# Two attention and two expert stages on one core: loads, last rows and router pieces moved where stages meet, a token's two result rows side by side, end sums on three engines

## The chip, the cores and the metric

The kernel runs on one core of a Trainium2 chip, as one launch. The metric is device time in microseconds (us). The profile adds one execution of the same program, taken apart by the hardware profiler. Five engines matter: TensorE (PE in the profile; its weight loads are PEld), VectorE (DVE), ScalarE (ACT), GpSimd (POOL) and SyncE (SP). SP, ACT and POOL also issue DMA transfers; each engine takes its instructions strictly in order, so an instruction that waits holds up all that stand behind it on that engine, DMA issues included.

## The reference

The input x is 8 batches of 512 tokens of width 256, in float32. Four layers follow, each with a residual:

```
x = x + attn_a(layernorm(x))     # 16 heads of 64, ALiBi, causal softmax, bias
x = x + ffn(layernorm(x))        # RMS norm, gate, top 2 of 8 experts, swiglu
x = x + attn_b(layernorm(x))     # 8 heads of 128, rotary, causal softmax
x = x + ffn(layernorm(x))        # the same expert weights again
```

In the expert layer each token's normed row h goes to the two experts with the largest gate logits. An expert computes a 256x512 product, a clipped swiglu and a 256x256 product. The residual of the inner layer is h's own input, so the layer's output is the token's x plus two expert rows, each times a softmax weight.

## The kernel before

Everything is float32 except the router's small one-hot tables. Tokens are laid on 128 partitions, so a batch has 4 token tiles of 128 rows.

**Attention** (class `Attention`, kinds "a" and "b") goes through 64 steps, a step being 2 heads of kind "a" or 1 head of kind "b" in one batch. A step of kind "a" (`step`, L503) issues on PE the scores of its own heads, then the transposes of the softmax rows of the step before (`turn`), the projections q and k of the step after, and the weighted sums of the step before (`average`). `extra(1)` and `extra(2)` are slots for other work: values, output projection, the next batch's norm, the router. Within one step the scores go from PSUM through DVE (L407: add the mask, take the row maximum), ACT (L417: exp and row sum), then a reciprocal on DVE and the scaling of the rows on DVE (the longest rows of a step; all rows in the very last step) and POOL (L434). The transposed rows come from PSUM through ACT, one of six banks through DVE (L457 and L459).

**Experts** (class `Experts`, kinds "f1" and "f2"). After each attention batch `norm`, `apply`, `turn_norm`, `gates`, `choose` and `count` make the router's input; `sorting` turns the choices into slots: all (token, choice) pairs are sorted by expert into blocks of 128 rows, padded, 71 blocks (TOTAL). The work has two stages: 41 blocks (FULL) hold pairs of batches 0 to 5 and can start before the router has seen batches 6 and 7; 30 blocks come after, and rows of batches 0 to 5 can lie in the first 55 blocks (TOUCHED). `tokens` (L891) computes for each slot which token's row to gather and to which row of the DRAM tensor `y_all` the result goes. `run` (L1049) is a software pipeline over n: at n it gathers block n+4 (`gather`, an indirect DMA on POOL), transposes the activations of block n-5, transposes the gathered rows of block n (`turn_rows`), does the first product of block n-2 (`first`) and the second of block n-6 (`second`, which ends with an indirect DMA on POOL that scatters 128 rows to `y_all`). The dictionary `aside` puts other pieces behind given values of n.

In `turn_rows` the transposed rows of the first AHEAD blocks are copied back into the tile they were gathered to; later blocks use a tile that shares its memory with the attention's output tile O, and so wait until the last output projection has read O.

**What sets the order.** PE's order is the program order. The other engines' instructions are put in order by a planner, which simulates the program with its own costs and takes the earliest written of those it holds ready; instructions marked `keep_in_program_order` stay in order. The order is fixed at build time: if a transfer takes longer on the chip than in the plan, the engine waits with what stands first.

**Where stages meet.** `layer` (L1133) spreads the router's pieces over the attention steps by batch, head group and slot. Pieces that fall behind the last batch are returned in `left`: the last step's transposes (`turn_last`), its weighted sum (`average`), two pieces of output projection, then norm, apply, turn_norm, gates, choose and count of batch 7. `flush` (L1195) puts these ten pieces at n = 0, 2, 2, 2, 3, 5, 8, 10, 12, 14 of the expert pipeline and the six sorting pieces of the second stage at 16, 18, 20, 22, 25, 28.

**Loads at the start.** Input DMAs stand on SP in the order of the code (L146 to L175): x of batch 0, wq, wk, alibi, bout, wv, wo, small tables, then 16 transfers of expert weights (`we`, 6 MB), sin. x of batch 1 is loaded by `fetch_a(0)` at slot (0, 1, 1), behind those. `fold_norm` scales the expert weights on POOL as they arrive (L243).

**Result rows.** `y_all` has two planes of 4096 rows, one for a token's first expert and one for its second, then spare rows for padding. `collect` (L1097) reads a tile's or half batch's rows back with one DMA from each plane (`read`, L1076); `add` (L1112) adds each row times its weight to x, one DVE instruction (L1118) per token tile and plane. For f1 the sums are made during attention b, one token tile per step; for f2, twelve half batches of batches 0 to 5 are summed from n = 61 on, and the four half batches of batches 6 and 7 at the very end, each followed by its store to the output (L1246).

## Time and profile before

| what | value |
|---|---|
| median of 3 runs | 2254.11 us (2252.29 to 2255.5) |
| the profiled execution's own time | 2239.6 us |
| span of that execution, first to last instruction | 2237.8 us |
| mean granted TensorE clock | 0.993 |
| PE busy | 2190.3 us, 98% of the span |
| DVE busy | 1586.9 us, 71% |
| ACT busy | 961.6 us, 43% |
| POOL busy | 967.1 us, 43% |
| DMA | 108.80 MB, mean 49 GB/s |

Times in the profile count from the start of the span. "Releaser" in brackets names what ended an engine's idle time before an instruction. Attention a lies at 0 to 927 us, f1 to 1175, attention b to 1976, f2 to the end. The PE clock row is the share of full clock that was granted.

### The profile page before, as it was taken

Reading aid. Unit: us, or ns where it says so; the run is one execution under the profiler, and the core shown is the slowest. Engines: PE = TensorE matmul, PEld = TensorE weight load, DVE = VectorE, ACT = ScalarE, POOL = GpSimd, SP = SyncE. Lnnn points to the kernel's source line nnn. Section 1 sums busy time; section 2 is a strip of 40 time slices with the busy share of each in tenths; the row PEclk is TensorE's granted clock in tenths of the full one; section 3 lists DMA queues with packets and bytes.
Section 4 is the critical chain, followed back from the end, with each engine's and each line's share of the span. In section 5 each row is a group of like instructions: output and inputs, shape, how many; then the busy total and the mean of one; then the engine's idle time right before and its main releaser. Section 6 shows DMA issues by size and latency. Waiting matters only on the chain.

```text
span 2237.8 us, 33567 instructions
## 1 busy us (share of the span) xinstructions
PE 2190.3 (98%) x10513; PEld 1429.2 (64%) x10513; DVE 1586.9 (71%) x4817; ACT 961.6 (43%) x2784; POOL 967.1 (43%) x1337
## 2 busy tenths in 40 slices
PE   8999999999999999999999999999999999999995
PEld 5666666666666666656666666666666666665663
DVE  4566666666666687687787676777777678968768
ACT  4555555555555555323324334434444433333331
POOL 5443434243433333266654343333434343356662
PEclk9999999999999999999999999999999999999997
DMA  7100000000000000232220010100101010042237
GB/s 248 39 15 15 6 24 1 30 1 29 1 29 1 29 6 29 99 106 84 90 76 29 10 39 10 39 29 19 48 6 43 6 34 1 19 139 78 85 101 252
DMA packets 78382, 108.80 MB, mean 49 GB/s; under 512 B 9568, under 2 KB 64000, under 8 KB 78208
## 3 DMA queue, kind: packets, MB, share of 16 engines
q1 hardware_dynamic: 62656, 67.58, 9.4%
q0 software_dynamic: 13632, 37.24, 5.4%
q8 instruction: 87, 1.43, 0.3%
q10 hardware_dynamic: 1920, 1.84, 0.3%
q14 instruction: 87, 0.71, 0.1%
HBM read 67.02 MB, written 39.60 MB: 48 GB/s over the span
## 4 chain that ended last, share of the span: by engine, by line
PE 88%; DVE 7%; issue 2%; ACT 1%; POOL 1%; SPq 1%; DMA 1%; DVEq 0%; ACTq 0%; POOLq 0%
PE pp_b L337 10%; PE hp_f L982 9%; PE pp_a L337 9%; PE op_a L476 6%; PE sp_b L395 6%; PE sp_a L395 6%; PE tp_a L449 6%; PE op_b L476 6%; PE yp_a L494 5%; PE yp_b L494 5%; PE vp_a L318 4%; PE y_f L1021 4%; PE vp_b L318 4%; PE tp_b L449 3%; PE gtp_f L953 1%
## 5 line engine op out<-in xcount | busy, mean ns | idle before, releaser
L417 ACT ACTIVATE S_a<-S_a,nm_a 128x512 f32<-128x512 f32 (+3 forms) x512 | 280.1, 548 | 313.7 <-DVE nm_a L407 309.9
L350 POOL TENSOR_TENSOR qk_b<-qk_b,rot_b 128x512 f32<-128x512 f32 x128 | 163.0, 1274 | 453.1 <-DVE qk_b L349 427.7
L376 POOL TENSOR_SCALAR ali_a<-alibi 128x512 f32<-128x512 f32 x128 | 79.3, 620 | 454.9 <-DVE nm_a L407 443.1
L982 PE MATMUL hp_f<-we,hT_f 128*128 x544 | 257.8, 596 | 4.3 <-DVE u_f L993 2.9
L417 ACT ACTIVATE S_b<-S_b,nm_b 128x512 f32<-128x512 f32 (+3 forms) x256 | 142.9, 559 | 241.1 <-DVE nm_b L407 233.4
L407 DVE CUSTOM_DVE_ANT_0 S_a<-sp_a,ali_a 128x512 f32<-128x512 f32 (+3 forms) x512 | 215.9, 487 | 30.7 <-PE sp_a L395 30.7
L434 POOL TENSOR_SCALAR S_a<-S_a,sum_a 128x384 f32<-128x384 f32 x378 | 203.1, 554 | 34.6 <-DVE sum_a L428 25.0
L1033 POOL DMA_INDIRECT y_f<-y_f,row_f x142 | 143.4, 1010 | 114.1 <-DVE y_f L1032 59.2
L407 DVE CUSTOM_DVE_ANT_0 S_b<-sp_b,mask 128x512 f32<-128x512 f32 (+3 forms) x256 | 119.4, 485 | 77.1 <-PE sp_b L395 76.7
L395 PE MATMUL sp_b<-qk_b 128*128 128x512 f32 (+3 forms) x512 | 169.7, 434 | 2.6 <-POOL qk_b L350 2.5
L449 PE MATMUL tp_a<-ident,S_a 128*128 128x128 f32 x1280 | 166.2, 276 | 5.4 <-DVE O_a L484 3.3
L939 POOL DMA_INDIRECT g_f<-h_all_f,token_f x142 | 144.4, 1017 | 59.4 <-issue 39.6
L449 PEld LDWEIGHTS tp_a<-ident,S_a 128*128 128x128 f32 x1280 | 141.3, 142 | 36.8 <-issue 21.3
L994 ACT ACTIVATE u_f<-u_f 128x256 f32<-128x256 f32 x142 | 59.2, 417 | 238.0 <-DVE u_f L993 179.5
L476 PE MATMUL op_a<-PT_a,V_a 128*64 128x384 f32 (+3 forms) x1024 | 156.0, 442 | 3.3 <-ACT S_a L417 2.2
L1021 PEld LDWEIGHTS y_f<-we,aT_f 128*128 128x128 f32 x568 | 108.8, 193 | 77.1 <-issue 59.6
L395 PE MATMUL sp_a<-qk_a 64*128 64x512 f32 (+3 forms) x1024 | 155.5, 443 | 0.9 <-DVE qk_a L354 0.9
L1021 PE MATMUL y_f<-we,aT_f 128*128 x568 | 148.6, 385 | 3.8 <-ACT aT_f L1012 3.7
L459 ACT COPY PT_a<-tp_a 128x512 f32<-128x512 f32 (+1 forms) x320 | 139.1, 496 | 29.4 <-PE tp_a L449 27.6
L476 PE MATMUL op_b<-PT_b,V_b 128*128 128x512 f32 (+3 forms) x512 | 148.7, 433 | 0.0
L993 DVE TENSOR_TENSOR u_f<-hp_f,be 128x512 f32<-128x512 f32 x142 | 98.2, 691 | 59.5 <-PE hp_f L982 20.5
L982 PEld LDWEIGHTS hp_f<-we,hT_f 128*128 128x128 f32 x544 | 92.7, 190 | 73.1 <-issue 66.3
(205 smaller groups left out, 4454.8 us busy)
## 6 DMA issues: line engine op xcount, KB each, us to landing
h_all_f<-hn_f SPq DMA_DIRECT2D x64, 128.0 KB
xm_f<-x_mid_f SPq DMA_DIRECT2D x16, 512.0 KB
yg_f<-y_f SPq DMA_DIRECT2D x32, 256.0 KB
yg_f<-y_f SPq DMA_DIRECT2D x56, 128.0 KB
we<-w_dram SPq DMA_DIRECT2D x8, 512.0 KB
x_mid_f<-x SPq DMA_DIRECT2D x8, 512.0 KB
x_mid_f<-xm_f SPq DMA_DIRECT2D x8, 512.0 KB
x<-x_in_dram SPq DMA_DIRECT2D x7, 512.0 KB
```

The lines of the kernel that those rows point to most:

```text
L318: nc.tensor.matmul(vp[:, k, :], lhsT=self.xT[b][:, c, t * P : (t + 1) * P], rhs=wv[:, c, q * 2 * P : (q + 1) * 2 * P], start=(c == 0), sto ...
L337: nc.tensor.matmul(pp, lhsT=w[:, c, g * P : (g + 1) * P], rhs=self.xT[b][:, c, :], start=(c == 0), stop=(c == NC - 1),)
L350: nc.gpsimd.tensor_tensor(qk[:, j, :], qk[:, j, :], rot, ALU.add)
L395: nc.tensor.matmul(sp[i][:, at[it] : at[it] + w], lhsT=qk[r, 0, it * P : (it + 1) * P], rhs=qk[r, 1, 0:w], start=True, stop=True,)
L407: nc.vector.tensor_tensor_reduce(out=s, in0=sp[i][:, at[it] : at[it] + w], in1=add[i][:, T - w : T], scale=scale, scalar=float(np.finfo(np ...
L417: nc.scalar.activation(s, s, AF.Exp, bias=nm[:, it : it + 1], scale=-1.0, accum_out=sums[:, it : it + 1],)
L434: eng.tensor_scalar(s, s, sums[:, it : it + 1], 1.0, ALU.mult, ALU.mult)
L449: nc.tensor.transpose(tp[:, o : o + P], S[:, S_OFF[it] + jt * P : S_OFF[it] + (jt + 1) * P], ident,)
L476: nc.tensor.matmul(op[i * cols : (i + 1) * cols, jt * P : T], lhsT=v[:, jt, c0 : c0 + cols], rhs=PT[i][:, P_OFF[jt] : P_OFF[jt] + T - jt * P],
L494: nc.tensor.matmul(yp[:, 0:D], lhsT=o[:, c, t * P : (t + 1) * P], rhs=wo[:, half * HALF + c, :], start=(c == 0), stop=(c == HALF - 1),)
L982: nc.tensor.matmul(hp, lhsT=h[:, c * P : (c + 1) * P], rhs=we_sb[:, bass.DynSlice(wat + c * 2 * FI, 2 * FI)], start=(c == 0), stop=(c == N ...
L1021: nc.tensor.matmul(yp, lhsT=aT[:, c * P : (c + 1) * P], rhs=we_sb[:, bass.DynSlice(wat + NC * 2 * FI + c * D, D)], start=(c == 0), stop=(c ...
```

## The change

It has these parts; no arithmetic of a result is changed but the place of a sum.

1. wq and wk of attention a are loaded in two pieces each: the first 256 columns of both, then alibi, then the other 768 columns.
2. x of batch 1 is loaded on SP before the expert weights; `fetch_a` goes on with batch 2.
3. In the last step of attention a the transposes of the step before come first, then the scores of the last step; then the extra slots and the weighted sum.
4. `flush` puts the ten pieces at 2, 4, 4, 4, 5, 7, 10, 12, 14, 17 and the sorting pieces at 18, 20, 22, 24, 26, 29, after both attentions. AHEAD goes from 3 to 5.
5. A token's two rows stand next to each other in `y_all` (rows 2t and 2t+1, spare rows from 8192 on). `tokens` computes this with one DVE instruction more, the gather's index before the scatter's. `collect` reads both rows with one DMA, in runs of 2 KB where two DMAs had runs of 1 KB.
6. For the last three of the twelve half batches and for the last four of f2, the second row's product goes to ACT and its sum to POOL; DVE keeps the first row. The last four reads go alternately to SP and ACT, one DMA each, where each had one on either queue.

```diff
-AHEAD = 3
+AHEAD = 5
...
+    def load_qk(first, end):
+        for k, w in enumerate((wq, wk)):
+            nc.sync.dma_start(
+                out=w[:, :, first:end],
+                in_=by_rows(a_qkv[:, k * INNER + first : k * INNER + end]),
+            )
+
+    load_qk(0, 2 * P)
     alibi_sb = load(const, [P, T], alibi, "alibi", "bias")
+    load_qk(2 * P, INNER)
...
     rank_sb = load(const, [P, NT, NE], rank, "rank")
+    X[1] = load_x(x_in[1], "x1")
...
-            if self.kind == "a":
+            if self.kind == "a" and not after:
+
+                turn(0, 0, 1, 2)
+                turn(1, 0, 1, 2)
+                for n in range(3):
+                    scores(n)
+                extra(1)
+                extra(2)
+            elif self.kind == "a":
...
+            nc.vector.scalar_tensor_tensor(
+                row_f, token_f, float(P), place, ALU.mult, ALU.add
+            )
+            nc.vector.tensor_scalar(token_f, mark, 96.0, 1.0, ALU.is_ge, ALU.mult)
+            nc.vector.scalar_tensor_tensor(
+                row_f, row_f, 2.0, token_f, ALU.mult, ALU.add
+            )
...
-                out=out, in_=self.y_all[first : first + n, :].rearrange("(t p) d -> p t d", p=P)
+                out=out,
+                in_=self.y_all[2 * first : 2 * (first + n), :].rearrange(
+                    "(t p k) d -> p t k d", p=P, k=2
+                ),
...
-            for k in range(2):
-                self.read(engines[k], b, got[:, k], k * PLANE + m * P, len(tiles) * P)
+            self.read(engine, b, got, m * P, len(tiles) * P)
...
                 for k in range(2):
-                    made = nc.vector.scalar_tensor_tensor(
-                        xs, got[:, k, n, :], self.R["w"][k][:, m : m + 1], xs, ALU.mult, ALU.add
-                    )
+                    row, w = got[:, n, k, :], self.R["w"][k][:, m : m + 1]
+                    if k and shared:
+
+                        nc.scalar.mul(row, row, w)
+                        nc.gpsimd.tensor_tensor(xs, xs, row, ALU.add)
+                        continue
+                    made = nc.vector.scalar_tensor_tensor(xs, row, w, xs, ALU.mult, ALU.add)
...
-        turns = (0, 2, 2, 2, 3, 5, 8, 10, 12, 14)
+        turns = (2, 4, 4, 4, 5, 7, 10, 12, 14, 17)
...
-        for n, piece in zip((16, 18, 20, 22, 25, 28), exp.sorting(1), strict=True):
+        for n, piece in zip((18, 20, 22, 24, 26, 29), exp.sorting(1), strict=True):
...
-    more += [((b, 1, 1), lambda b=b: fetch_a(b + 1)) for b in range(NB - 1)]
+    more += [((b, 1, 1), lambda b=b: fetch_a(b + 1)) for b in range(1, NB - 1)]
...
-        aside.setdefault(n + 4, []).append(lambda b=b, tt=tt: exp_b.add(b, tt))
+        aside.setdefault(n + 4, []).append(
+            lambda b=b, tt=tt, k=k: exp_b.add(b, tt, k >= len(halves) - 3)
+        )
...
-    for b, tt in last:
-        exp_b.collect(b, tt, "S", (nc.sync, nc.scalar))
+    for k, (b, tt) in enumerate(last):
+        exp_b.collect(b, tt, "S", (nc.sync, nc.scalar)[k % 2])
...
-        exp_b.add(b, tt)
+        exp_b.add(b, tt, True)
```

## The prediction

> **What bounds the kernel now.** I read the page first: PE works almost without a break, so only PE's work or its few gaps can be won, plus the ends of the span.
>
> ```profile
> PE 2190.3 (98%) x10513; PEld 1429.2 (64%) x10513; DVE 1586.9 (71%) x4817; ACT 961.6 (43%) x2784; POOL 967.1 (43%) x1337
> PE   8999999999999999999999999999999999999995
> PEclk9999999999999999999999999999999999999997
> ```
>
> The change takes no matmul away, so the 47.5 us in which PE is idle (2237.8 less 2190.3) and the time at a lowered clock are all there is to win. The table by stretches says where they are (columns: stretch, length, busy us of PE, PEld, DVE, ACT, POOL, granted clock, DMA share, GB/s).
>
> ```profile
> 0.00:30.00 30.00, 24.80 (x109) 16.02 (x110) 14.12 (x59) 12.47 (x37) 16.57 (x38) 1.00 0.94 316
> 30.00:60.00 30.00, 26.96 (x137) 15.59 (x136) 15.25 (x54) 13.61 (x41) 16.70 (x29) 0.94 0.48 146
> 920.00:960.00 40.00, 37.43 (x182) 23.86 (x183) 26.54 (x74) 15.31 (x44) 15.77 (x19) 0.96 0.33 108
> 1180.00:1900.00 720.00, 717.12 (x3057) 481.97 (x3057) 530.99 (x1454) 288.76 (x759) 278.46 (x349) 1.00 0.07 23
> 2200.00:2238.00 38.00, 14.16 (x46) 9.03 (x44) 31.80 (x77) 3.63 (x11) 7.97 (x8) 0.69 0.77 249
> ```
>
> Attention b is closed (2.9 us open of 720); the start, the meeting of attention a and f1, and the end are open. Third, the timeline of each. At the start, SP, DVE and PE:
>
> ```profile
> 31.16 0.37 SPq L134 DMA_DIRECT2D x<-x_in_dram  x1
> ...
> 39.63 0.75 DVE L253 BATCH_NORM_STATS2 st_a<-x 128x6 f32<-128x256 f32 x2 [5.30 <-DMA x<-x_in_dram]
> ...
> 42.01 1.04 PE L449 MATMUL tp_a<-ident,S_a 128*128 128x128 f32 x6 [2.56 <-DVE O_a L484]
> 43.23 3.26 PE L337 MATMUL pp_a<-xT_a,wq_a 128*128 128x512 f32 x4 [0.17 <-DVE nm_a L407]
> ```
>
> x of batch 1 is issued at 31.16 behind the expert weights and lands at 39.6. The planner had put its statistics ahead of DVE's next work, so DVE stands 5.30 us with scores and copies behind, and PE stands too, then runs slowly (3.26 us for four matmuls that take 1.88 later).
>
> At 920, ACT and PE:
>
> ```profile
> 926.26 1.32 ACT L459 COPY PT_a<-tp_a 128x512 f32<-128x512 f32 x3
> ...
> 926.88 1.07 PE L476 MATMUL op_a<-PT_a,V_a 128*64 128x512 f32 x2 [2.23 <-ACT S_a L417]
> 928.28 3.82 PE L476 MATMUL op_a<-PT_a,V_a 128*64 128x512 f32 x14 [0.34 <-issue]
> ```
>
> The last step's scores come first, so ACT's exps (921.89 to 926.3) stand ahead of the copies that the weighted sum needs.
>
> At the end PE stops at 2217.8 and DVE adds rows without a break, 33 times 0.46 us, to 2234.34; the last store and its landing take 3.46 us more.
>
> ```profile
> 2219.20 15.14 DVE L1118 SCALAR_TENSOR_TENSOR xm_f<-yg_f,wt_f,xm_f 128x256 f32<-128x256 f32 x33
> 2222.59 2.11 ACTq L1078 DMA_DIRECT2D yg_f<-y_f  x4
> ```
>
> **The change part by part**, against the profiled execution's own 2239.6 us (14.5 below the median, which I take off at the end).
>
> *Batch 1's x ahead of the expert weights.* Scores of step 2 start at 35.84, those of step 3 at 55.40: 19.56 us. The same kind of step in batch 4 takes 13.89 (chain, 466.39 to 480.28). Excess 5.67, gap and slow clock together: it goes if x is there in time. x takes the place of the first expert weight, whose first use on POOL starts on its landing, at 20.93. Its eight statistics instructions take 1.75 us (39.63 to 41.38). In DVE's order they should now fall after step 0's scores (end 19.18): waiting to 20.93 and ending at 22.68, they put the 1.54 us of reciprocals and scalings that stood at 20.55 to 22.09 and the q/k copy (22.37) to 24.2 to 24.9. PE's next scores need that copy by 23.99, so PE waits +0.9. Bounds: 0, if they stand behind the copy; +5.7, if they stand ahead of step 0's scores, where DVE is free from 14.4 (that is rival B).
>
> Late next are the expert weights, 512 KB later, at 316 GB/s 1.7 us. POOL takes them in order, and its softmax scaling stands behind: PE already waits 0.99 for it at 27.41 and 0.19 at 38.45. Bounds 0 (at 29.16 POOL does seven scalings in 5.08 us with no wait) and +1.7; I take +0.6, nearer the unwaited row.
>
> *wq, wk in pieces.* PE waits 0.53 for wk at 11.69; its wait for wq is covered by xT, ready at 9.17. Gain 0.5. Two SP issues more, 0.45 each, move all behind by 0.9; SP is held there by full queues (one issue lasts 6.15 us), so nothing. alibi lands earlier than 12.32; the first scores wait for PE, not for it. Start in sum: -5.7 +0.9 +0.6 -0.5 = -4.7.
>
> *Last step of attention a, pieces two blocks later, AHEAD 5.* From 919.88 to the first activation transpose at 949.93 PE needs 30.05 us. The work at full clock: scores 2.36, twenty transposes 2.3, weighted sum 2.31, five row transposes 1.1, last transposes 2.2, three first products 5.16, weighted sum 2.3, output projection 7.0: 24.7. Excess 5.3. In the new order ACT copies the transposes before its exps, and the first weighted sum follows the scores without a wait, to about 926.9. Then PE has only row transposes, whose copies stand behind the exps on ACT; these end 6.4 after the scores' start, now 922.2: 928.6, copy to 929.1. A gap of about 1.6 replaces 2.57, and the scaled rows (up to 931.1) are then covered by the first product. Block 3 and 4 now keep their gather tile until their first products, so the gather of block 8 on POOL waits for that, with the row norm's 5.05 us of POOL work (947.46 to 952.5) beside it: +0.5, bounds 0 and +1.3 (one gather issue with its pause: 0.95 and 0.30). A slow clock after the gap: bounds 0 and +2.4 (what 926.88 to 932.04 lost: 5.16 less 0.34 less 2.37), taken +0.7. New excess 2.8, so -2.5; bounds -3.7 and 0.
>
> On that clock the skill has a rule. The Trainium skill's page "TensorE: Matmul & The Clock Gate", section "What's actually happening", lets the clock fall to half after an idle window of about 3.4 us. The rows here show slow matmuls after gaps of 2.56 and 2.23 us, below that; by the page the +0.7 would be 0 and the time 0.7 lower, by the rows it stands.
>
> *The same pieces after attention b.* PE loses 0.83 at 1977.56 and 0.69 at 1985.32. Later pieces cover both with first products, but row transposes 1 and 2 then wait for gathers issued 1.25 apart: -0.4, bounds -1.5 and +0.7. The later sorting costs nothing while its last piece, n = 29, lies before the gather of block 41 at n = 37: eight blocks of 3.02 us.
>
> *Rows side by side.* One read less per tile on SP (0.4 us); SP waits there for other reasons 541.7 us. DVE's extra router instruction is 0.2 us, twice, inside PE's work. The scatters keep their size. In attention b the sums lie beside a full PE: 0, bounds in rival D.
>
> *End sums.* Of DVE's 33, fourteen go: 14 x 0.46 = 6.4 us less. POOL does 14 sums instead; the nearest row, its 128x256 add, is very even:
>
> ```profile
> L299 POOL TENSOR_TENSOR x<-x,bout x32: 717/722/732, 13.7 to 795.6; 128x256 f32<-128x256 f32 x32
> ```
>
> ACT's products (0.42, row L994) lie beside. But the two engines slow each other: L1118 takes 0.48 alone and up to 0.81 beside POOL's scaling in attention b. POOL's 14, from about 2222, take 10.1 at 0.72 and 14.7 at 1.05 (0.72 plus the same 0.33), so they end between 2232.1 and 2236.7 against DVE's 2234.34: -2.2 to +2.4. Data bounds it as well: the last reads are issued at 2222.6, and with stores 3 MB at 370 GB/s last to 2230.7. I take 0.84 a sum, nearer the undisturbed row because DVE is idle part of that time: -0.7.
>
> A rule of the skill speaks against this part. "GPSIMD Engine Reference", section 4.1 "Engine selection", says to keep elementwise work on VectorE, GpSimd being about twice as slow with two inputs. The rows show 0.72 against 0.48, 1.5 times; by the page's factor a sum would be an estimated 0.96, POOL would end at 2235.4, and this part would cost 1.1 rather than gain 0.7.
>
> Sum: -4.7 -2.5 -0.4 -0.7 = -8.3: 2231.3 for the profiled execution, and 2254.1 - 8.3 = **2245.8** for the median.
>
> **The rivals.**
>
> B, the stall only moves: the statistics stand ahead of step 0's scores or POOL's scalings wait for late weights, and the start gains nothing. For it: the planner was 5 us too early with this very transfer. Against it: DVE is busy from 15.80 to 19.18, and the transfer now comes early. -3.6: 2250.5.
>
> C, the meetings don't gain: PE waits at 928 as long as it did, and POOL ends the kernel at 2236.7. For: ACT still does nine exps first, and L1118's 0.81. Against: one gap less on ACT's order. -4.7 +2.4 = -2.3: 2251.8.
>
> D, slower: attention b's 28 tile sums wait for their one 256 KB read. For: a sum starts 2.2 us after its read's issue (1309.99 to 1312.17), so little is to spare; behind it on DVE stand the scores' reductions, for which PE waits. Against: DVE shows no wait for these reads, has 189 of 720 us free, and one issue comes earlier than two. At 0.5 us a tile, 14 us: 2259.8. It decides from (8.3 + 4.5)/28 = 0.46 us a tile.
>
> **How the numbers follow.** About 0.2% (4.5 us) can be told from no change. Forecast 0.62, its own range 2241 to 2249.6, faster. B 0.16 and C 0.09 lie within 0.2%: 0.25. D 0.13, slower. The range reaches from near the forecast's bounds (start -6.2, then -3.7, -1.5, -2.2: -13.6, 2240.5) over B and C to 2256; D and little else is left out.
>
> **What would show it.** DVE's 5.30 us wait for x gone, and less than 2 us in its place; step 2 to 3 in about 14 us; no wait of the weighted sum for ACT near 924, and the first activation transpose some 2.5 us nearer to the last scores; in the tail 19 sums on DVE, 14 on POOL of 0.72 to 1.05 each, the last ending some 14.5 us after the last expert row leaves DVE (before: 2219.29 to 2234.34, 15.05). The prediction is wrong if DVE waits over 4 us for x at any place, if POOL's sums pass 1 us, or if DVE waits for reads in attention b.

## The result and the profile after

The changed kernel is slower: median 2262.0 us against 2252.3 for the kernel before in the same set of runs, ratio 1.0046 (95% interval 1.0034 to 1.0058), so +10 us where -8.3 was forecast. A second set, with other runs of both, gave 1.0037 (1.0023 to 1.0050). Times of the kernel before differ between sets by up to 1.1% (medians 2227 to 2252 us), and its first profiled execution (2239.6) lay 10 us and more under its timed ones, so 2263.7 less 2239.6 overstates the loss: ratios are compared within a set only.

The page of the kernel after, busy engines and slices of the span:

```profile
PE 2195.1 (97%) x10513; PEld 1431.7 (63%) x10513; DVE 1585.9 (70%) x4807; ACT 966.5 (43%) x2798; POOL 971.9 (43%) x1351
PE   8999999999999999989999999999999999998994
```

PE does the same 10513 matmuls in nearly the same busy time (2190.3 before); what is lost is idle time again. The table by stretches (columns as before the change: length, busy us of PE, PEld, DVE, ACT, POOL, granted clock, DMA share, GB/s):

```profile
0.00:30.00 30.00, 22.43 (x82) 14.01 (x84) 13.33 (x51) 8.01 (x22) 13.22 (x32) 0.83 0.95 320
30.00:60.00 30.00, 30.00 (x171) 18.81 (x172) 17.06 (x62) 19.19 (x60) 20.65 (x36) 1.00 0.43 142
920.00:960.00 40.00, 37.01 (x181) 23.45 (x180) 28.80 (x80) 16.39 (x48) 14.86 (x19) 1.00 0.29 94
1180.00:1900.00 720.00, 717.16 (x3045) 481.61 (x3044) 528.49 (x1450) 290.22 (x762) 280.13 (x351) 1.00 0.07 24
2200.00:2262.00 62.00, 31.44 (x115) 19.79 (x113) 45.10 (x101) 14.73 (x42) 26.63 (x30) 0.77 0.68 223
```

The stretch from 30 to 60 is now closed, as the forecast wanted, but the one before it does 82 matmuls instead of 109, at a clock of 0.83. So the start is shifted, not shortened. For the whole span I cut both traces at the same events (first matmuls of a group). "Again" is a second profile of each kernel unchanged, in runs whose medians for before were 2227.2 and 2227.8:

| stage, us | before | after | before again | after again | again, difference |
|---|---|---|---|---|---|
| to the scores of step 56 | 813.0 | 811.8 | 812.3 | 811.6 | -0.8 |
| to block 3's first product (meeting) | 137.4 | 133.4 | 137.3 | 133.4 | -4.0 |
| f1, to attention b's first transposes | 200.7 | 211.3 | 195.9 | 200.7 | +4.8 |
| attention b, to its last scores | 819.8 | 823.0 | 821.2 | 819.6 | -1.6 |
| to block 3's first product of f2 | 24.5 | 24.8 | 23.5 | 22.8 | -0.7 |
| f2, to PE's last matmul | 222.5 | 231.0 | 214.6 | 218.8 | +4.2 |
| tail | 20.0 | 26.6 | 22.6 | 25.9 | +3.3 |
| span | 2237.8 | 2261.9 | 2227.4 | 2232.7 | +5.3 |

The meeting gained more than forecast, f1 and f2 gave it back twice, the tail lost and the start barely moved. (Attention b takes 819.6 to 823.0 in profiles of either kind, without a pattern that follows the change.)

**The start.** PE's and POOL's timelines of the kernel after:

```profile
10.53 2.24 PE L286 MATMUL xtp_a<-ident,xn_a 128*128 128x128 f32 x8 [4.60 <-DVE xn_a L273]
13.34 3.78 PE L348 MATMUL pp_a<-xT_a,wq_a 128*128 128x512 f32 x4 [0.57 <-DVE xT_a L317]
```

```profile
5.28 0.20 POOL L267 TENSOR_SCALAR rs_a<-mv_a 128x4 f32<-128x4 f32 x1 [3.09 <-DVE mv_a L265]
7.87 0.62 POOL L387 TENSOR_SCALAR ali_a<-alibi 128x512 f32<-128x512 f32 x1 [2.40 <-DMA alibi<-alibi_dram]
8.57 1.04 POOL L268 TENSOR_TENSOR rs_a<-rs_a,mhalf 128x4 f32<-128x4 f32 x1
```

And the same places in the kernel before:

```profile
6.95 1.41 PE L275 MATMUL xtp_a<-ident,xn_a 128*128 128x128 f32 x8 [0.31 <-DVE xn_a L262]
```

```profile
5.40 1.05 POOL L257 TENSOR_TENSOR rs_a<-rs_a,mhalf 128x4 f32<-128x4 f32 x1
```

In POOL's order the first ali_a (alibi times a head's slope) now stands between the two instructions of the norm's reciprocal root and waits 2.40 us for alibi. The root begins at 8.57 (5.40 before), PE waits 4.60 us for xn_a, the normed rows (0.31 before), its next products are slow (3.78 us where the same four take 1.95 before), and the first scores come at 20.43 instead of 14.55. Step 2 to 3 then takes 13.89 us instead of 19.56, so the x stall is gone and step 3's scores come at 54.27 (before 55.40).

**The meeting and f1.** PE at the meeting, and the waits of PE from 940 to 1180 (columns: who waits for whom, us in total, times, longest). Of the names, gtp_f is the transposing of a block's gathered rows g_f, hp_f a block's first product, u_f its swiglu on DVE, atp_f and aT_f its transposed activations, inv_f and col_f a product and a table of the router's sorting, xtp_b the first transposes of attention b:

```profile
920.69 2.43 PE L406 MATMUL sp_a<-qk_a 64*128 64x512 f32 x16
923.05 2.37 PE L487 MATMUL op_a<-PT_a,V_a 128*64 128x512 f32 x16
...
927.47 1.98 PE L1006 MATMUL hp_f<-we,g_f 128*128 x4 [1.24 <-ACT g_f L985]
...
931.70 1.88 PE L1006 MATMUL hp_f<-we,g_f 128*128 x4
...
944.76 0.38 PE L1031 MATMUL atp_f<-ident,u_f 128*128 128x128 f32 x2
```

```profile
PE hp_f L1006 <- ACT aT_f L1036: 3.0, 1, 3.0
PE hp_f L1006 <- DVE u_f L1017: 2.7, 3, 2.1
PE inv_f L900 <- DVE col_f L885: 1.8, 2, 1.4
PE xtp_b L286 <- DVE xn_b L273: 1.7, 2, 1.4
PE gtp_f L977 <- DMA g_f<-h_all_f,token_f: 1.6, 1, 1.6
```

From the last scores to the first activation transpose PE needs 24.07 us (30.05 before), with one wait of 1.24 where I expected 1.6. The last scores come 2.0 later than before, counted from step 56, because the transposes now stand ahead of them: together -4.0. Behind it stand new waits: PE for the router's sorting (inv_f for col_f), and for the gather of a block (g_f).

**The tail.** The last sums on DVE and POOL, and POOL's closing DRAIN (an instruction of its sequencer at the program's end) in the groups by line (shortest, median, longest in ns; first start to last end):

```profile
2247.14 2.61 DVE L1150 SCALAR_TENSOR_TENSOR xm_f<-yg_f,wt_f,xm_f 128x256 f32<-128x256 f32 x4 [3.04 <-DMA yg_f<-y_f]
2251.23 2.61 DVE L1150 SCALAR_TENSOR_TENSOR xm_f<-yg_f,wt_f,xm_f 128x256 f32<-128x256 f32 x4 [1.47 <-DMA yg_f<-y_f]
```

```profile
2251.84 3.26 POOL L1148 TENSOR_TENSOR xm_f<-xm_f,yg_f 128x256 f32<-128x256 f32 x4 [0.83 <-ACT yg_f L1147]
```

```profile
L1368 POOLq DRAIN  x3: 45/107/7112, 2254.0 to 2261.6; - x3
```

DVE waits for the last reads now, and POOL's DRAIN runs from 2254.0 for 7.11 us, to 2261.1. The last store was issued at 2255.13; the span ends 6.75 us after it, where before it ended 3.45 us after. (In the first pair of profiles the last sum also ends later after PE's last matmul, 19.8 us against 16.5; in the second pair both take 19.1, and the drain is the whole +3.3.)

### The profile page after: what moved, and what is told of

Read it like the earlier page. It is cut to its first block, busy times and chain, and to the rows that moved or that the text cites. A ratio compares the mean times of both kernels' runs of the same rounds, so it can differ in the third digit from the quotient of the medians.

```text
span 2261.9 us, 33497 instructions
## 1 busy us (share of the span) xinstructions
PE 2195.1 (97%) x10513; PEld 1431.7 (63%) x10513; DVE 1585.9 (70%) x4807; ACT 966.5 (43%) x2798; POOL 971.9 (43%) x1351
## 4 chain that ended last, share of the span: by engine, by line
PE 87%; DVE 7%; issue 2%; DMA 1%; ACT 1%; POOL 1%; another core or an unknown queue 0%; DVEq 0%; SPq 0%; POOLq 0%; ACTq 0%
PE pp_b L348 9%; PE pp_a L348 9%; PE hp_f L1006 8%; PE sp_a L406 6%; PE op_a L487 6%; PE tp_a L460 6%; PE sp_b L406 6%; PE op_b L487 6%; PE yp_a L505 5%; PE yp_b L505 5%; PE vp_a L329 5%; PE vp_b L329 4%; PE y_f L1045 4%; PE tp_b L460 3%; PE gtp_f L977 1%
## 5 line engine op out<-in xcount | busy, mean ns | idle before, releaser
L418 DVE CUSTOM_DVE_ANT_0 S_a<-sp_a,ali_a 128x512 f32<-128x512 f32 (+3 forms) x512 | 215.9, 487 | 30.5 <-PE sp_a L406 30.0
L445 POOL TENSOR_SCALAR S_a<-S_a,sum_a 128x384 f32<-128x384 f32 x378 | 202.2, 551 | 34.2 <-DVE sum_a L439 25.9
L487 PE MATMUL op_a<-PT_a,V_a 128*64 128x256 f32 (+3 forms) x1024 | 153.5, 439 | 0.7 <-DVE PT_a L468 0.7
L1017 DVE TENSOR_TENSOR u_f<-hp_f,be 128x512 f32<-128x512 f32 x142 | 98.1, 691 | 62.9 <-PE hp_f L1006 24.8
```

What stands on the lines that cost most here:

```text
L418: nc.vector.tensor_tensor_reduce(out=s, in0=sp[i][:, at[it] : at[it] + w], in1=add[i][:, T - w : T], scale=scale, scalar=float(np.finfo(np ...
L445: eng.tensor_scalar(s, s, sums[:, it : it + 1], 1.0, ALU.mult, ALU.mult)
L487: nc.tensor.matmul(op[i * cols : (i + 1) * cols, jt * P : T], lhsT=v[:, jt, c0 : c0 + cols], rhs=PT[i][:, P_OFF[jt] : P_OFF[jt] + T - jt * P],
```

## The experiments

The first theory of most runs is that each place of loss above has its own cause and that undoing it gives that amount back; the rivals are named at each run.

**Both kernels again**, no edit.

> The kernel before, unchanged, for a second profile of it. Its profiled execution took 2239.6 us, its timed ones 2249.6 to 2255.5, while the changed kernel's profiled execution lies among its timed ones. Theory 1: the first profile is of an unusually quick execution, by some 12 us; then a second one takes 2249 to 2256, and the comparison of stages shows where those 12 us lie (my guess: in f1 and f2, where PE waits for transfers and for DVE). Theory 2: profiling itself makes this kernel quicker; then the second profiled execution is near 2240 again. The ratio of times is 1.000 within 0.001.

> The changed kernel, unchanged, beside the other runs of this set. Theory 1: the change costs a fixed sum that does not depend on the chip: from the stages of the first set (kernel before against kernels that share stages with the changed one) -0.8 at the start, -6.0 between the last scores of attention a and block 3's first product, +3.1 in f1, -0.7 after attention b, +4.8 in f2, +4.2 in the tail, +4.6 us in all, a ratio of 1.002. Rival: as first measured, 1.0046, about +10 us; then f1 and f2 lose more than 8 us on this chip too, as in the first profile (12 and 8.5).

The kernel before against itself: 1.0002 (0.9993 to 1.0011). Its profiled execution (2229.2) lies among its timed ones (2224.9 to 2230.3), so profiling does not make it quicker: the first profile was of an unusually quick execution. The kernel after: 1.0037, nearer the rival's 1.0046, but f1 and f2 lose 4.8 and 4.2 us and not over 8. Their stages are in the table. So a difference of 0.1% can be trusted within a set; between sets the ratio of one and the same kernel moved by up to 0.24% (a_gap_dve below), so parts that were measured in different sets are known only to about that.

**The start: alibi back behind whole wq and wk**, in the kernel after.

```diff
-    load_qk(0, 2 * P)
+    load_qk(0, INNER)
     alibi_sb = load(const, [P, T], alibi, "alibi", "bias")
-    load_qk(2 * P, INNER)
```

> The changed kernel with wq and wk whole and alibi behind them, as before; x of batch 1 stays ahead of the expert weights. Theory 1: the first scores come at 14.5 again, 5.9 us earlier, since POOL's slope table no longer stands, waiting for alibi, inside the norm's chain; but DVE's order has batch 1's statistics right behind the first two score reductions, and x lands at about 20.9 there, so DVE then waits some 4 us from 16.6, and the scores of step 3 come at 52 to 53 (changed kernel: 54.27): 1 to 2 us less than the changed kernel in all. Rival: x of batch 1 is there in time and the whole 5.9 us are gained, scores of step 3 at 48.4. If alibi's place has nothing to do with the late start, the first scores stay at 20.4.

Ratio 1.0035 (1.0022 to 1.0047): no gain. PE and DVE:

```profile
14.84 2.43 PE L405 MATMUL sp_a<-qk_a 64*128 64x512 f32 x16 [0.88 <-DVE qk_a L364]
...
28.11 4.63 PE L405 MATMUL sp_a<-qk_a 64*128 64x512 f32 x16 [3.76 <-DVE qk_a L364]
```

```profile
17.32 0.08 DVE L417 DVE_READ_ACCUMULATOR2_ANT nm_a<- 128x1 f32 x1
21.36 0.75 DVE L263 BATCH_NORM_STATS2 st_a<-x 128x6 f32<-128x256 f32 x2 [3.96 <-DMA x<-x_in_dram]
```

The first scores are back at 14.84. (The edit also makes wq and wk whole again; that alibi was the cause is read from POOL, where the root begins at 5.42 again with no ali_a ahead of it.) But now rival B's mechanism appears in the same kernel: the planner put batch 1's statistics behind two score reductions of step 0, DVE stands 3.96 us for x, and step 3 begins at 55.20 again (52 to 53 expected). The stall that the early load was to remove had only been hidden behind the delay that alibi made.

**x still earlier, ahead of wv**, with wq, wk and alibi loaded as before, old positions and all end sums on DVE.

```diff
+    X[1] = load_x(x_in[1], "x1")
     wv = load(wpool, [P, NC, INNER], by_rows(a_qkv[:, 2 * INNER : 3 * INNER]), "wv_a", "wv")
...
-    X[1] = load_x(x_in[1], "x1")
     we_sb = const.tile([P, NE * W_COLS], F32, tag="we", name="we")
```

> The changed kernel with pieces at the positions of before, all end sums on DVE, wq, wk and alibi loaded as before, and x of batch 1 ahead of wv, two transfers earlier than in the change. Theory: the place of x decides through the planner. DVE's order then has batch 1's statistics ahead of its first q/k copy; x takes the place of wv and should land near 15, so the copy waits some 1 to 2 us where a_start's reductions waited 3.96; first scores at 15.5 to 16.5, no later wait for x, scores of step 3 at 50.5 to 52.5 (kernel before on this chip 54.4 to 54.8), step 56 at 808 to 810 (before 812). wv lands 2 us later, with its first use at 19.7 uncertain. In all 2 to 4 us under the kernel before: 0.998 to 0.999. Rival: the same 4 us of wait again, because the planner takes x for landed about 4 us before it is, wherever it stands; then 1.000, scores of step 3 at 54.

Ratio 1.0016 (1.0007 to 1.0025), first scores at 24.51 and step 3 at 58.49: a worse start. DVE:

```profile
15.35 0.75 DVE L263 BATCH_NORM_STATS2 st_a<-x 128x6 f32<-128x256 f32 x2 [7.47 <-DMA x<-x_in_dram]
16.41 0.68 DVE L316 COPY xT_a<-xtp_a 128x512 f32<-128x512 f32 x1
```

The planner moved the statistics further ahead than the data came: now they stand before batch 0's own transposes are copied. In all three orders in which DVE stands for x (5.30, 3.96 and 7.47 us), the planner took x for landed some 4 us or more too early. That points to another cure, tried next.

**The kernel before with the statistics made late.** Batch 1's statistics get a first instruction that reads the q/k tile of step 6; no load is moved and nothing else of the change is in it.

```diff
-    def ln_stats(b, key):
+    def ln_stats(b, key, after=None):
...
+        if after is not None:
+            nc.vector.tensor_copy(st[:, :, 0], after)
...
-            self.xn[b] = ln_stats(b, self.kind)
+            late = self.kind == "a" and b == 1
+            self.xn[b] = ln_stats(b, self.kind, self.qk[0, 6][:, 0, 0:NT] if late else None)
```

> The kernel before with one thing changed: batch 1's statistics are tied, by a copy of 128x4, to the q/k of step 6, so that they can stand in DVE's order only when x has long landed; all loads stay as they were. Theory 1: in each start the stall comes from the planner, which puts the statistics into DVE's order some 4 us before x lands, wherever x stands in the queue; taken out of there, the step from scores 2 to 3 is 14 us instead of 19, scores of step 3 at 49 to 50.5, step 56 some 4.5 to 5.7 us earlier, ratio 0.9975 to 0.998. Rival: another wait takes its place, POOL's weight scalings, for which PE waited 0.99 already: 1 to 3 us less, 0.999.

Ratio **0.9979 (0.9970 to 0.9989)**, the one version that beats both kernels. DVE and PE:

```profile
84.21 0.51 DVE L253 COPY st_a<-qk_a 128x4 f32<-128x4 f32 x1 [0.77 <-ACT qk_a L355]
```

```profile
35.87 2.43 PE L398 MATMUL sp_a<-qk_a 64*128 64x512 f32 x16
...
50.89 1.45 PE L398 MATMUL sp_a<-qk_a 64*128 64x512 f32 x6
```

Step 2 to 3 takes 15.02 us instead of 19.56, and step 56 comes at 808.46; in the five other profiles that have the loads of before at this place it comes at 811.95 to 813.58. So the stall was worth most of what I had priced (4.5 of 5.67 us from step 2 to 3), and its cause was the planned place of an instruction, not the place of the load. This kernel was run in one set only.

**Positions put back**, in the kernel after (start, last step's order, AHEAD 5, rows and end sums stay).

```diff
-        turns = (2, 4, 4, 4, 5, 7, 10, 12, 14, 17)
+        turns = (0, 2, 2, 2, 3, 5, 8, 10, 12, 14)
...
-        for n, piece in zip((18, 20, 22, 24, 26, 29), exp.sorting(1), strict=True):
+        for n, piece in zip((16, 18, 20, 22, 25, 28), exp.sorting(1), strict=True):
```

> The changed kernel with the router pieces at the positions of before (0, 2, 2, 2, 3, 5, 8, 10, 12, 14 and sorting at 16, 18, 20, 22, 25, 28); AHEAD stays 5. Theory 1: the positions themselves cost f1 and f2 their 12 and 8 us in the profile, because count and sorting stand closer together there (17 to 18 where it was 14 to 16; 24, 26, 29 where it was 22, 25, 28) and DVE does them in a run ahead of expert work that PE waits for: 8 to 20 us less than the changed kernel, PE's waits for u_f (2.11, 2.22) and col_f (1.40 twice) gone, f1 from block 3's first product to the first transpose of attention b in 200.7 us as before (changed kernel: 211.3). Rival: AHEAD 5, through the gather of block 8 (1.63), and code or transfers that arrive late at random: then 0 to 3 us less, with f1 still above 207. The meeting after attention a: 0.7 us in f1's favour or against it.

1.0019 (1.0010 to 1.0028): 0.18%, some 4 us, where 8 to 20 were expected from the first profile. The meeting is back at 136.7, f1 at 195.85 and f2 at 214.3, nearly as in the kernel before. So the new positions cost what f1 and f2 lose, and that is more than the meeting gains. PE's wait for the gather is gone too although AHEAD is still 5, so AHEAD by itself doesn't make it.

**The positions alone**, in the kernel before: the order of the last step of attention a, AHEAD = 5, turns and sorting, as in the change.

```diff
-AHEAD = 3
+AHEAD = 5
...
-        turns = (0, 2, 2, 2, 3, 5, 8, 10, 12, 14)
+        turns = (2, 4, 4, 4, 5, 7, 10, 12, 14, 17)
```

> The kernel before with one part of the change: the last step's order, AHEAD 5, and all pieces at the changed positions. Theory 1, from the profiles of the first chip: -4.0 to block 3's first product, +4.8 in f1, -0.7 after attention b, +4.2 in f2: +4.3 us, 1.002, and more where f1 and f2 hold further waits (up to 1.0035 where the kernel before takes 2240 to 2250 us). Rival: the positions cost only together with the shared sums at the end of f2: 1.000.

1.0025 (1.0015 to 1.0035), so +5.6 us by themselves: the meeting takes 133.7, f1 211.5 and f2 232.0. Another run of that set (the rows alone, below) has f1 205.6 and f2 224.2 with the old positions. PE's waits from 940 to 1180 name the gather and the sorting again, and more waits for u_f:

```profile
PE hp_f L990 <- DVE u_f L1001: 3.4, 3, 2.2
PE gtp_f L961 <- issue: 2.0, 1, 2.0
PE gtp_f L961 <- DMA g_f<-h_all_f,token_f: 1.6, 1, 1.6
PE inv_f L889 <- DVE col_f L874: 1.2, 1, 1.2
```

**The sorting's pieces three blocks apart at the end again**, at the new positions (in the change its last two steps are 2 and 3 blocks).

```diff
-        for n, piece in zip((18, 20, 22, 24, 26, 29), exp.sorting(1), strict=True):
+        for n, piece in zip((19, 21, 23, 25, 28, 31), exp.sorting(1), strict=True):
```

> The changed kernel with the sorting pieces at 19, 21, 23, 25, 28, 31, so that the distances are those of before (16, 18, 20, 22, 25, 28) or one more, the ten other pieces as changed. Theory 1: what f1 and f2 lose with the new positions is mainly the distance that fell from 3 to 2 blocks (24, 26 for 22, 25), in which DVE must build one pair's tables: PE's waits for col_f (1.4 and 0.4) go in both stages, 3 us less than the changed kernel. The wait for the gather of block 8 (1.6 each) stays, since POOL makes the router's norm before it. Rival: the lateness of all pieces counts, not their distance; then the waits for col_f stay or move to another table, and the time is that of the changed kernel or more.

1.0017 (1.0008 to 1.0026) against 1.0037. PE's waits from 940 to 1180, of the kernel after in the same set and of this one:

```profile
PE inv_f L900 <- DVE col_f L885: 1.8, 2, 1.4
PE gtp_f L977 <- DMA g_f<-h_all_f,token_f: 1.6, 1, 1.6
PE xtp_b L286 <- DVE xn_b L273: 0.3, 1, 0.3
```

```profile
PE gtp_f L977 <- DMA g_f<-h_all_f,token_f: 1.6, 1, 1.6
PE xtp_b L286 <- DVE xn_b L273: 0.3, 1, 0.3
```

The waits for col_f are gone and f1 falls from 200.65 to 198.41. So the place of the pieces to each other counts, not only that the last lies before its reader: one piece builds a pair's tables on DVE, the next multiplies them on PE. Of the waits, the gather's is left: PE waits 1.61 us for it, and the first and second product behind it take 2.93 and 1.80 us instead of 1.88 and 1.03 (granted clock 0.65 from 954.8 to 958). That is enough for the 2.6 us that f1 still takes over the kernel before (195.86).

**Another buffer for the gather of blocks 8 to 11**, in the kernel after.

```diff
+                tag, bufs = ("S", 4) if m == 2 * ROWS else ("qk", 2)
...
-                    [P, ROWS, D], F32, tag="qk", name=f"g_{self.kind}_{m}"
+                    [P, ROWS, D], F32, tag=tag, bufs=bufs, name=f"g_{self.kind}_{m}"
```

> The changed kernel with the tile of blocks 8 to 11's gathered rows in other memory, which is free at the meeting, so that their gathers need not wait for block 3's first product and stand ahead of the router's norm on POOL. Theory 1: PE's wait of 1.6 us for that gather in f1 and in f2 goes, with the slow matmuls behind it 3 to 5 us less than the changed kernel (ratio to the kernel before 1.0015 to 1.003). Rival: the norm then comes 4 to 5 us later on POOL, its rows later to the router, and the later pieces, which stand close as it is, cost what was gained: 0 to 1 us less.

1.0057 (1.0043 to 1.0071): worse. POOL in the kernel after (second profile), and here:

```profile
945.94 0.20 POOL L267 TENSOR_SCALAR rs_f<-mv_f 128x4 f32<-128x4 f32 x1 [17.49 <-DVE mv_f L265]
951.01 0.31 POOL L618 TENSOR_TENSOR rs_f<-rs_f,rs_f 128x4 f32<-128x4 f32 x1
...
951.73 1.08 POOL L963 DMA_INDIRECT g_f<-h_all_f,token_f  x1 [0.41 <-issue]
```

```profile
932.25 1.10 POOL L964 DMA_INDIRECT g_f<-h_all_f,token_f  x1 [2.62 <-DVE u_f L1021]
...
947.13 0.20 POOL L267 TENSOR_SCALAR rs_f<-mv_f 128x4 f32<-128x4 f32 x1 [9.82 <-DVE mv_f L265]
```

With its own tile the gather goes out 19 us earlier and PE's 1.6 us wait for it is gone, so the buffer and POOL's queue (the norm's 5.4 us and a 17.49 us wait ahead of it) made that wait. They did not make it alone: in the kernel before the gather of block 8 also goes out behind the norm, at 953.10, but PE turns to its rows only at 958.35, 5.3 us later, and with positions put back it is 5.3 us as well. In the kernel after PE is ready for them 1.4 us after the issue: the output projection, whose rows the norm waits for, now stands two blocks nearer to block 8. And here other waits appear, the largest behind attention b:

```profile
PE op_b L487 <- ACT PT_b L470: 4.7, 1, 4.7
PE atp_f L1032 <- DVE u_f L1018: 2.4, 1, 2.4
```

From the last scores of attention b to block 3's first product of f2 this kernel takes 30.4 us; a_gap_dve, which keeps the old tile, takes 24.9 in the same set. So the loss is larger than the rival's price, and not where the rival put it: in f1 the norm starts no later than in the kernel after's second profile (134.4 us after step 56 in both). The new tile lies in the memory that the softmax rows and u_f use too; that this is why PT_b comes late is likely, but no run shows it. What the gather's wait alone is worth in the whole time stays open.

**All end sums on DVE**, in the kernel after.

```diff
-            lambda b=b, tt=tt, k=k: exp_b.add(b, tt, k >= len(halves) - 3)
+            lambda b=b, tt=tt, k=k: exp_b.add(b, tt)
...
-        exp_b.add(b, tt, True)
+        exp_b.add(b, tt)
```

> The changed kernel with all end sums on DVE, as before; the reads stay one DMA each, alternately on SP and ACT. Theory 1: POOL's closing drain ends 5.96 us after POOL's last instruction in both profiles (2220.53 to 2226.49, hidden; 2255.11 to 2261.07, exposed), where the last store has landed at 2257.3; and ACT's products, which wait for reads, hold up activations that PE needs (2.65 us at 2227.91). Without POOL and ACT the end is again 3.4 us behind the last sum, and PE's last matmul some 2 to 3 us earlier: 5 to 7 us less than the changed kernel. Rival: DVE has 14 sums of 0.46 us more and becomes the bound of the end, as in the kernel before: 0 to 2 us less. Second rival: the last reads' landing (2251.2) bounds the end whoever adds: then 1.9 us of sums and 3.4 us follow it, 2256.5 for the span, 5 us less, but with PE no earlier.

1.0018 (1.0009 to 1.0027). The tail is 22.4 (25.9 with shared sums, 22.6 before). The last sum ends 19.2 us after PE's last matmul, against 19.1 with shared sums (on POOL; DVE's own last ends at 17.9) and 19.1 in the kernel before: the sharing had gained nothing there, and lost 3.3 us after the last store. PE's last matmul, which theory 1 had expected 2 to 3 us earlier, is not: f2 takes 219.3 (218.8 with shared sums).

**One sum on POOL**, in the kernel before: the very last sum of f2.

```diff
+                    if self.kind == "f2" and k == 1 and m == NB * NT - 1:
+                        nc.scalar.mul(row, row, w)
+                        nc.gpsimd.tensor_tensor(xs, xs, row, ALU.add)
+                        continue
```

> The kernel before with one single change: the very last of the 33 end sums (second row of batch 7's last tile) is a product on ACT and a sum on POOL. Theory 1: POOL's closing drain ends 5.96 us after POOL's last instruction whatever that was, and the span 0.8 later; the sum itself costs 0.3 us (0.72 after DVE's last against 0.46), the end moves from 3.4 behind the last sum to 6.8: +3.7 us, ratio 1.0016. Rival: the drain is long for another reason (scatters under way at the time); then POOL's drain is short here, and the time is +0.3 us, ratio 1.000.

1.0022 (1.0013 to 1.0031), so +4.9 us (2.9 to 6.9) for one instruction of 0.72 us; the drain behind the last store, below, accounts for 3.3 of them. POOL's sum, and its DRAIN:

```profile
2219.87 0.72 POOL L1121 TENSOR_TENSOR xm_f<-xm_f,yg_f 128x256 f32<-128x256 f32 x1 [13.44 <-DVE xm_f L1123]
```

```profile
L1341 POOLq DRAIN  x3: 45/107/6727, 2219.8 to 2227.1; - x3
```

And the DRAIN of the kernel before (first profile), where POOL's last work had ended at 2220.53, 13.8 us ahead of DVE's last sum:

```profile
L1338 POOLq DRAIN  x3: 45/107/7160, 2219.3 to 2237.6; - x3
```

In 19 of the 20 profiles the long DRAIN ends 5.95 to 5.97 us after POOL's last instruction, in the other (best4) 6.18: in the kernel before at 2226.5, hidden under DVE's sums; here at 2226.57, with the last store issued at 2220.63 and the end at 2227.37, 6.74 us later.

**Rows side by side alone**, in the kernel before: the new row numbers, one read a tile, the last reads on SP and ACT in turn.

```diff
-            for k in range(2):
-                self.read(engines[k], b, got[:, k], k * PLANE + m * P, len(tiles) * P)
+            self.read(engine, b, got, m * P, len(tiles) * P)
```

> The kernel before with one part of the change: a token's rows side by side, one read per tile, the gather's index ahead of the scatter's, the last four reads alternately on SP and ACT. Theory 1: it costs nothing and gains nothing, as predicted: 1.000, attention b's length within 1.5 us of the other profiles' (795.4 to 797.1 from its first to its last step). Rival: the missing part of the sums of this study (kernels without the later positions and without the shared sums still stand at 1.000, not below, although their start is 1 us shorter) sits here: 1.0005 to 1.001.

0.9993 (0.9981 to 1.0006). Attention b from first to last step takes 797.07 us (795.60 in the first profile of before, 797.08 in the second). DVE waits for none of the reads there, in this kernel or in the kernel after. Rival D did not happen.

**Combinations.** best1 puts positions and end sums of the kernel after back; a_gap_dve joins the two edits "three blocks apart" and "sums on DVE", and was run in two sets; best5 is a_gap_dve with old positions in f2; best4 is best3's start with old positions in f2 and the spaced sorting in f1; best7 joins a_gap_dve, alibi back, the other gather buffer and the late statistics.

> The changed kernel with the router pieces at the positions of before and all end sums on DVE; kept are the start, the last step's order, AHEAD 5 and the rows side by side. Theory 1, the stages add: start -0.8, meeting after attention a -2.6, f1 0, meeting after attention b -0.1, f2 -0.3, tail -0.1: 3.9 us under the kernel before, a ratio of 0.998. Rival: parts undone together give less than their sum, because another wait takes their place: 0.999 to 1.001.

> The changed kernel with the sorting pieces at 19, 21, 23, 25, 28, 31 and all end sums on DVE; start, last step, the ten other pieces, AHEAD and rows stay as changed. Theory: the two losses are separate and add. Against the kernel before, the changed kernel stood at 1.0037, with the wider distances alone at 1.0017 (-0.0020), with DVE's sums alone at 1.0018 (-0.0019): both give 0.9998. Rival: they overlap, since both act on the end of f2; then 1.001.

> The changed kernel with the wider sorting distances and all end sums on DVE, a second time, since its first result (1.0036) was 0.0038 over the sum of its parts (0.9998), which were measured on another chip. Theory 1: the sum of the changed positions depends on the chip; then the result follows the kernel before: about 0.9998 where that takes 2227 us, about 1.0036 where it takes 2240 us. Rival: the first result was chance, and it is 0.9998 to 1.001 on either.

> As the other kernel of this set, but after attention b all pieces at the positions of before. In the profiles of one chip the changed positions, with the wider distances, gain 3.3 us before block 3's first product of f1 and lose 2.5 in f1, and gain 0.6 and lose 2.0 to 3.1 at f2, where the gather of block 8 stands behind the router's norm on POOL: 1.4 to 2.5 us less than the other kernel, 0.999 of the kernel before. Rival: the wait for that gather is no loss in f2; then the same as the other kernel.

> As the other kernel of this set, but after attention a the ten pieces at the changed positions and the sorting at 19, 21, 23, 25, 28, 31; after attention b as before. From the profiles of this chip, step 56 to block 3's first product takes 133.4 us with the changed positions and 136.7 with those of before, and f1 198.4 against 195.9: 0.8 us less than the other kernel if the stages add, 0.9975 to 0.9985. Rival: what the earlier pieces gain at the meeting is given back in f1 to the last: the same as the other kernel.

> The changed kernel with wq, wk and alibi as before, batch 1's statistics tied to step 6 as in the first kernel of this set, the sorting at 19, 21, 23, 25, 28, 31, the gather tile as in the second, all end sums on DVE. If the stages add: start -5.5, from step 56 to block 3 of f1 -4, f1 +1, after attention b -0.6, f2 +1.5 to +2.5, tail 0: 5 to 8 us less than the kernel before, 0.9965 to 0.998. Rival: the start gains, the later positions cost as much more again on this chip as they did where two kernels of this kind stood at 1.0036 and 1.000: 0.999 to 1.000.

| kernel | ratio to before | 95% interval |
|---|---|---|
| best1 | 1.0002 | 0.9993 to 1.0011 |
| a_gap_dve | 1.0036 | 1.0022 to 1.0050 |
| a_gap_dve, second set | 1.0012 | 1.0003 to 1.0021 |
| best5 | 1.0000 | 0.9990 to 1.0010 |
| best4 | 1.0029 | 1.0019 to 1.0040 |
| best7 | 1.0019 | 1.0010 to 1.0028 |

With positions and sums put back, the rest of the change comes to nothing (best1): start, last step's order, AHEAD and rows are neutral together. a_gap_dve should be 0.9998 if the two edits simply add up (1.0037 less 0.20% less 0.19%); it gave 1.0036 and 1.0012, so they don't, and why stays open. Part of it is f2: in the set where a_gap_dve gave 1.0036, putting back the positions behind attention b alone gave 1.0000 (best5; f2 221.7 us instead of 225.8), so the wider sorting had not mended them there. best7 reaches step 56 at 807.93, the earliest of all, and loses that and more later (30.5 us behind attention b, with the other gather buffer, and 209.6 in f1): only b_late, the kernel before with the late statistics, kept the gain of the start. Neither is the spread between sets explained: f1 of the same code takes 195.9 us in one set and 200.7 or more in another, with more and longer waits at each hand-over.

## Why the prediction was wrong

Three steps failed: that the later positions cost f1 and f2 next to nothing, that alibi's place doesn't matter at the start, and that only the last store's landing follows the last sum. Part by part, with the forecast in us:

- **Meeting of attention a and f1, -2.5.** Right in mechanism: no wait of the weighted sum for ACT, a gap of 1.24 in place of 2.23, no slow clock. Under-sized: -4.0, just past the bound of -3.7, and that leaves out the gather of block 8, whose wait falls behind this stretch.
- **"The later sorting costs nothing while its last piece ... lies before the gather of block 41."** This step failed. I looked at the last piece's distance to its reader only. The pieces also read each other, and where two stand two blocks apart instead of three PE waits for col_f inside the sorting: 1.4 and 0.4 us of waits, 2.2 us of f1, 0.20% of the whole time in the sets of the second profiles.
- **Gather of block 8, +0.5.** Mis-sized: PE waits 1.6 for it in f1, above my +1.3, and 1.6 again in f2, which I had not priced at all, because POOL issues the gather behind the norm, and with the projection two blocks later PE comes to block 8 only 1.4 us after that (5.3 us before). In the second profile the wait costs 1.8 us more by slow matmuls (4.75 us where 2.91 is usual, granted clock 0.62). Positions in all were forecast at -2.9 and measured at +0.25% alone, +5.6 us. That error of 8.5 us is the largest.
- **Start, -4.7.** The x stall went as priced (13.89 us from step 2 to 3), with no wait over 4 us of DVE for x in the kernel after itself. "alibi lands earlier ... the first scores wait for PE, not for it" failed: alibi earlier changed POOL's order, and its wait moved into the norm's chain, +5.9 us to the first scores. And rival B's condition, the statistics ahead of step 0's scores, was met (ahead of all but two of their reductions) as soon as alibi was put back. Measured -0.8 to -1.2 at step 56, and 1.0002 on the whole with the rows (best1).
- **End sums, -0.7.** POOL's price was right: 0.85 us a sum on average (848 ns, 14 sums) against 0.84, and DVE's beside it 0.65 (2.61 for four) instead of 0.46. The rule that I had weighed, from the Trainium skill's "GPSIMD Engine Reference", section 4.1 "Engine selection", is right in its advice here, with a factor of 1.5 alone (0.72 to 0.48, in which DVE makes the product too) and 1.3 beside each other (0.85 to 0.65), and not two. But neither row nor rule was what cost: the term left out is what follows on POOL after its last instruction. I took the landing of the last store as the only thing behind the sums; the DRAIN of 5.96 us lay hidden in the trace of before and comes to light when POOL works to the end: +3.3 us in the tail.
- **Rows, 0, and after attention b, -0.4.** Right: 0.9993, and -0.65 in the second profiles (+0.4 in the first).
- **The clock.** The prediction set the rows above the rule of "TensorE: Matmul & The Clock Gate", section "What's actually happening" (about 3.4 us idle). The gap that I priced stayed at 1.24 us and cost no clock (1.00 granted, 1.98 us for four matmuls). Longer ones did, still below that figure: 1.61 us in the second profile of the kernel after (though not 1.63 in the first, where the clock stayed at 1.00), and in f1 of the first one of 3.02 us, with a granted clock of 0.64 from 969.5 to 974. Four matmuls of the same shape take 1.88 us where no wait stands ahead (931.70 above).

```profile
969.51 2.59 PE L1006 MATMUL hp_f<-we,hT_f 128*128 x4 [3.02 <-ACT aT_f L1036]
```

  That 3.02 us wait is absent from the second profile of the same kernel, and its cause is not known.

Summed from the runs of single parts: positions +0.25%, end sums +0.19%, start about 0, rows -0.07%: +0.37%, against +0.46% and +0.37% measured. In us, positions +5.6 where -2.9 was forecast, end sums some +4.2 where -0.7, start about 0 where -4.7: these three carry the way from -8.3 to some +10. That they add up here may be luck, since in other combinations the parts did not.

## What to carry to other kernels

When work is moved in a planned order, follow every queue that it passes and every buffer that it now keeps longer, not only its last reader: the gain at the meeting was real and was lost blocks later, at a gather and a sorting that the move had touched. Where an engine stands for a transfer, first see whether its instruction was simply planned too early; tying that one instruction to later data won 0.21% in the set where it was tried, and moving the load won nothing. Look at what each engine does after its last instruction before giving it work at the end.

## What the runs showed of the hardware

- POOL's closing DRAIN ends 5.95 to 5.97 us after POOL's last instruction in 19 of 20 profiles (6.18 in best4), behind the issue of a scatter as behind a sum; one add of 0.72 us moved to POOL's end costs 0.22%.
- A 128x256 f32 sum takes POOL 0.72 us alone and 0.85 on average beside DVE's sums, and DVE 0.46 and 0.65: each slows the other.
- Four matmuls took 2.59 instead of 1.88 us after a wait of 3.02 us (granted clock 0.64), and 3.05 after one of 1.61 in the second profile (0.62); in the first, 1.98 after one of 1.63 (1.00).
